# Identity products in the planned waits of TensorE, in a four-layer graph network

## The chip, the cores and the metric

The kernel runs on one core of a Trainium2 chip. The metric is the device time of one execution in microseconds, as the median of several runs. Five engines work side by side in the core: TensorE (matmul), VectorE (DVE), ScalarE (ACT), GpSimd (POOL) and SyncE (SP), which here only issues DMAs. They run their own instruction streams in order and wait for each other with semaphores.

## The reference

32 graphs of 512 nodes with 128 features pass through four layers; each is a graph network behind a layer norm and a ReLU, added to its input. Cut to what is computed:

```python
# layer 0
h = relu(layernorm(x)); A = adj + I; r = rowsum(A) ** -0.5
x = x + leaky_relu((r[:, None] * A * r[None, :]) @ (h @ W) + b, 0.01)
# layer 1
h = relu(layernorm(x))
x = x + tanh(concat(adj @ elu(h @ Win.T + bin), elu(h @ Wnode.T + bnode),
                    adj.T @ elu(h @ Wout.T + bout)) @ Wupd.T + bupd)
# layer 2: four steps, f0 = relu(layernorm(x)), with f1, f0 stashed and concatenated
f = tanh(concat(l2norm_rows(adj) @ (f @ ws + bs), f @ wn + bn,
                l2norm_cols(adj).T @ (f @ wd + bd)) @ wu + bu)
x = x + f4
# layer 3: a gated update
h = relu(layernorm(x)); m = tanh(adj @ (h @ Wmsg.T + bmsg))
r, z, n = gates(m, h)
x = x + (1 - z) * n + z * h
```

All is in float32, inputs, weights and products.

## The kernel before

A graph is a batch. Its adjacency matrix lies in SBUF twice, as it is (`a`) and transposed (`aT`), each as four chunks of 128 partitions by 512 columns. Aggregations are four accumulating products of 128x512, one for each chunk; weight products have 128 or 256 columns. Matrices that hang only on the weights are folded once, at the start (`ps_fold`, `ps_foldb`), and two-by-two blocks of products are written with seven instead of eight (`ps_seven`).

The kernel doesn't issue instructions while it walks through the layers. `program(b)` and `setup()` only record operations: engine, a duration assumed for it, what it reads and writes, and a closure that emits it. `Plan.order()` then simulates the five engines with these durations: an operation is ready when what it hangs on has ended, and each engine takes the ready one with the smallest key, which is a due time of its batch (28 us apart, `PERIOD`) less the length of the chain behind it. `order()` also hands out the eight PSUM banks and the SBUF slots. Its result is one list; emitting it in that order gives each engine its instruction stream. The real semaphores are put in later, from the data, so a stream's order is the plan's, but its times are the chip's.

The first batches run through the chain of layers with little else to do; from the third batch's start TensorE always has several batches to choose from. At the end, the last two batches are alone again. In batches 0 to 2, 30 and 31 the transposed h is made by TensorE (`transposed`, L483 with ACT's copy at L485); in the others by a DMA bounce (`turned`, copy at L488).

Names and lines that the text uses:

- Every matmul made by the helper `mm` has line L295, so tiles tell them apart: `ps_fold` and `ps_foldb` (weight folds, copied out by ACT at L353 and L371), `ps_agg` (aggregations), `ps_lin` (layer 0's weight, from `agg`, which ACT copies at L632), `ps_sd` (pairs of projections; DVE adds their bias at L522), `ps_node`, `ps_upd`, `ps_msg`, `ps_gate`. L566 is `ps_seven`.
- A layer norm is `bn`, `mv` and `v` on DVE (L419, L421, L422), the power on POOL (L435), `nb` on DVE (L443) and four activations `h` on ACT (L447), one for each 128 rows.
- Layer 0 ends with DVE's `z` (L637), `y` (L640) and `xr` (L642). Row sums come from ACT (`sq`, L607) and DVE's L609; sums of squares from ACT's L686, DVE's L689 and POOL's power L690, which goes through DRAM (`bounce`, L695, and `spaced`, L699) and ACT's `rows` (L704) into DVE's scaling of `aT` and `a` (L708).
- Layer 1's `rep` is ACT's exponential (L659) and DVE's L660 and L662; its outputs are copied by ACT as `agg_in` (L667) and `agg_out` (L671).
- Each step of layer 2 ends with ACT's tanh `f` (L737).
- The identity `ident` is made by POOL first thing; the products of the change read it.

Of the kernel before, what the change touches and what calls it, by code (L numbers as in the profile page):

```python
# [13 lines left out]
F32 = mybir.dt.float32  # L14
# [4 lines left out]
P = 128  # L19
B, N, D = 32, 512, 128  # L20
# [71 lines left out]
class Plan:  # L92
# [62 lines left out]
    def order(self):  # L155
        for i, o in enumerate(self.ops):
            o.waits, o.ready = len(o.after), 0.0
            for other in o.after:
                other.next.append(o)
            for buf in o.bufs:  # L160
                buf.left += 1
        for i, o in reversed(list(enumerate(self.ops))):
            o.tail = max([o.us + o.land] + [self.lag(o, n) + n.tail for n in o.next if n.batch == o.batch])

            due = o.batch * PERIOD if o.batch < B - 1 else (B - 2) * PERIOD + ENDING
            o.key = (due - o.tail + o.later if o.rank is None else o.rank - 1e6, i)
        free = {k: list(range(n)) for k, n in self.places.items()}
        unfinished = {}
        for o in self.ops:
            unfinished[o.batch] = unfinished.get(o.batch, 0) + 1  # L170
        queues, idle_at = {e: [] for e in self.SIGNAL}, dict.fromkeys(self.SIGNAL, 0.0)
        events, seq = [], 0

        def event(at, what, o=None):
            nonlocal seq
            seq += 1
            heapq.heappush(events, (at, seq, what, o))

        for o in self.ops:
            if not o.waits:  # L180
                event(0.0, "ready", o)
        done = []
        while events:
            now = events[0][0]
            while events and events[0][0] <= now + 1e-9:
                _, _, what, o = heapq.heappop(events)
                if what == "ready":
                    heapq.heappush(queues[o.engine], (o.key, o))
                elif what == "end":
                    for buf in o.bufs:  # L190
                        buf.left -= 1
                        if not buf.left and buf.kind in free:
                            free[buf.kind].append(buf.slot)
                    unfinished[o.batch] -= 1
                    if not unfinished[o.batch]:
                        del unfinished[o.batch]
            for e, queue in queues.items():
                if idle_at[e] > now + 1e-9:
                    continue
                held, o = [], None  # L200
                while queue and o is None:
                    item = heapq.heappop(queue)
                    new = [x for x in item[1].bufs if x.slot is None and x.kind in free]
                    older = item[1].batch - min(unfinished)
                    if any(len(free[x.kind]) < len([y for y in new if y.kind == x.kind]) + older * self.kept.get(x.kind, 0) for x in new):
                        held.append(item)
                        continue
                    o = item[1]
                    for x in new:
                        x.slot = free[x.kind].pop(0)  # L210
                for item in held:
                    heapq.heappush(queue, item)
                if o is None:
                    continue
                done.append(o)
                idle_at[e] = now + o.us
                event(now + o.us, "idle")
                event(now + o.us + o.land + self.SIGNAL[e], "end", o)
                for n in o.next:
                    n.waits -= 1  # L220
                    n.ready = max(n.ready, now + self.lag(o, n))
                    if not n.waits:
                        event(n.ready, "ready", n)
        assert len(done) == len(self.ops), "the plan does not end"
        return done


@with_exitstack
def gnn_stack(
# [11 lines left out]
    nc = tc.nc  # L241
    const = ctx.enter_context(tc.tile_pool(name="const", bufs=1))
    sb = ctx.enter_context(tc.tile_pool(name="sb", bufs=1))
    psum = ctx.enter_context(tc.tile_pool(name="psum", bufs=1, space=bass.MemoryType.PSUM))
    dram = ctx.enter_context(tc.tile_pool(name="dram", bufs=1, space=bass.MemoryType.DRAM))
    plan = Plan(sb, psum, {"bank": 8, "s2": 32, "s4": 6, "s8": 10}, {"bank": 1, "s2": 5, "s4": 0, "s8": 1})
# [7 lines left out]
    ident = const.tile([P, P], F32, name="ident")  # L254
# [133 lines left out]
    def program(b):  # L388
# [422 lines left out]
        for k in range(0, NC, w2):  # L811
            s, part, cols = slice(k, k + w2), set(range(k, k + w2)), w2 * D

            def step(dst, fn, reads, engine="DVE"):
# [12 lines left out]
            op("SP", 0.4, lambda s=s: nc.sync.dma_start(out[b][:, s, :], xo.ap()[:, s, :]),  # L827
               [(xo, part)], [], kb=cols / 2)

    setup()  # L830
    for b in range(B):
        program(b)
    with tc.manual_schedule():
        for o in plan.order():
            o.emit()


# [41 lines left out]
```

## Time and profile before

| what | value |
|---|---|
| median of 5 runs | 2330.21 us (2329.8 to 2331.43) |
| the profiled execution's own time | 2329.8 us |
| its span, first to last instruction | 2328.0 us |
| TensorE busy | 2294.4 us (99%) |
| DVE, ACT, POOL busy | 1520.0, 934.8, 287.6 us |
| mean granted TensorE clock | 0.996 |
| clock in 20 to 60 us, 60 to 100 us | 0.85, 0.98 |
| TensorE busy in 0 to 20 us, 20 to 60 us | 8.64, 31.68 us |
| TensorE's waits of over 2 us in all | the first fold for its load 10.7, transpositions for h 5.1 |

The profile is one execution, recorded by the hardware. A row of the timeline has start and duration in us, the engine, the line, the operation with its tiles and shapes, how many records were merged, and in brackets how long the engine had been idle before and what ended that. TensorE's ends are modelled: records overlap, so the pace of a stream is read from start to start. A float32 product has two matmul records (a transposition one), so "x8" is four products. A row of the windows has the stretch, its length, busy time and count of records of TensorE, its weight loads, DVE, ACT and POOL, then the granted clock, the DMA engines' mean share and GB/s.

### The profile page before, as it was taken

What the parts mean: (1) busy time and instruction counts of PE and PEld (TensorE: products, weight loads), DVE (VectorE), ACT (ScalarE), POOL (GpSimd) and SP (SyncE); (2) the same over time, 40 slices, a digit from 0 to 9 for tenths busy, and PEclk for the clock granted to TensorE, in tenths of its full rate; (3) what the DMA queues carried; (4) which work ended last, traced back from release to release, by engine and by line L of the source; (5) the groups of instructions that cost most, each with busy time, mean ns of one, the idle gap of its engine ahead of it and who ended that gap; (6) DMA issues with size and microseconds to landing.
All of it is one profiled execution on the core that took longest, in us unless ns stands there. A gap on an engine that the chain in (4) does not pass through costs nothing.

```text
span 2328.0 us, 28035 instructions
## 1 busy us (share of the span) xinstructions
PE 2294.4 (99%) x9594; PEld 1437.9 (62%) x9594; DVE 1520.0 (65%) x4124; ACT 934.8 (40%) x2018; POOL 287.6 (12%) x218
## 2 busy tenths in 40 slices
PE   6999999999999999999999999999999999999998
PEld 4666666566665666666666666666656666666665
DVE  5556567666676776757766676666767667576754
ACT  7323434344343444434444333443434444344512
POOL 2001101111110111111111111111001111111101
PEclk9999999999999999999999999999999999999999
DMA  6202222323323133222233223232231332323100
GB/s 219 78 1 86 68 74 80 109 64 100 98 84 109 47 108 105 91 86 88 75 101 100 77 88 109 64 100 93 82 114 48 109 97 93 92 63 114 50 5 10
DMA packets 127295, 196.63 MB, mean 84 GB/s; under 512 B 18352, under 2 KB 75184, under 8 KB 127152
## 3 DMA queue, kind: packets, MB, share of 16 engines
q1 hardware_dynamic: 126864, 194.71, 26.8%
q8 instruction: 76, 1.25, 0.2%
q14 instruction: 67, 0.55, 0.1%
q10 hardware_dynamic: 288, 0.13, 0.0%
HBM read 157.95 MB, written 36.83 MB: 84 GB/s over the span
## 4 chain that ended last, share of the span: by engine, by line
PE 90%; DVE 4%; DMA 3%; issue 2%; ACT 1%; POOL 1%; SPq 0%; ACTq 0%; DVEq 0%; POOLq 0%
PE ps_agg L295 60%; PE ps_seven L566 12%; PE ps_sd L295 9%; PE ps_upd L295 3%; PE ps_gate L295 2%; PE ps_msg L295 1%; PE ps_node L295 1%; PE ps_lin L295 1%; DMA turned<-turn_turned 0%; DMA aT<-in_adjt 0%; DVE bn L419 0%; ACT h L447 0%; DMA a<-in_adj 0%; POOL inv L690 0%; POOL sc L435 0%
## 5 line engine op out<-in xcount | busy, mean ns | idle before, releaser
L295 PE MATMUL ps_agg<-aT,sd 128*128 128x512 f32 x1024 | 510.0, 594 | 1.4 <-DVE sd L544 0.9
L295 PE MATMUL ps_agg<-a,sd 128*128 128x512 f32 x1024 | 489.4, 593 | 0.0
L435 POOL TENSOR_TENSOR sc<-v,neg_half 128x4 f32<-128x4 f32 (+1 forms) x128 | 173.7, 1358 | 1623.6 <-DVE v L422 1049.2
L295 PEld LDWEIGHTS ps_agg<-a,sd 128*128 128x128 f32 x1024 | 181.7, 190 | 158.3 <-issue 148.8
L447 ACT ACTIVATE h<-xr,nb,sc 128x128 f32<-128x128 f32 x384 | 158.2, 482 | 295.7 <-DVE nb L443 292.0
L295 PE MATMUL ps_agg<-f,w_sb 128*128 128x512 f32 x448 | 229.7, 595 | 0.0
L295 PEld LDWEIGHTS ps_agg<-aT,sd 128*128 128x128 f32 x1024 | 177.8, 191 | 74.8 <-issue 61.7
L295 PE MATMUL ps_sd<-w_sb,f 128*128 128x256 f32 x768 | 222.0, 382 | 1.4 <-ACT f L485 1.3
L566 PEld LDWEIGHTS ps_seven<-t_sb,s 128*128 128x128 f32 x1128 | 164.2, 191 | 67.9 <-issue 56.2
L295 PEld LDWEIGHTS ps_sd<-w_sb,f 128*128 128x128 f32 x768 | 137.7, 192 | 107.5 <-issue 86.4
L522 DVE TENSOR_TENSOR sd<-ps_sd,rf_sb 128x512 f32<-128x512 f32 x128 | 88.3, 690 | 149.9 <-PE ps_sd L295 149.2
L566 PE MATMUL ps_seven<-t_sb,s 128*128 128x128 f32 x1128 | 177.2, 275 | 0.0
L737 ACT ACTIVATE f<-ps_agg,cf_sb 128x512 f32<-128x512 f32 x128 | 87.4, 683 | 145.3 <-PE ps_agg L295 145.2
L295 PE MATMUL ps_agg<-aT,rep 128*128 128x512 f32 x256 | 130.9, 593 | 1.2 <-DVE rep L662 0.9
L295 PE MATMUL ps_agg<-a,rep 128*128 128x512 f32 x256 | 130.7, 592 | 0.0
L295 PE MATMUL ps_agg<-aT,msg 128*128 128x512 f32 x256 | 127.6, 593 | 0.0
L566 PEld LDWEIGHTS ps_seven<-w_sb,f 128*128 128x128 f32 x512 | 83.5, 191 | 55.7 <-issue 47.1
L690 POOL TENSOR_TENSOR inv<-stat,neg_half 128x8 f32<-128x8 f32 x32 | 64.7, 2021 | 372.1 <-DVE stat L689 372.1
L592 DVE TENSOR_TENSOR ev<-ps_seven,ev 128x512 f32<-128x512 f32 x94 | 64.7, 688 | 65.1 <-PE ps_seven L566 63.7
L295 PE MATMUL ps_agg<-aT,h 128*128 128x256 f32 (+2 forms) x384 | 99.7, 380 | 0.0
L607 ACT ACTIVATE sq<-a 128x512 f32<-128x512 f32 x128 | 79.9, 624 | 47.0 <-DMA a<-in_adj 45.4
L295 PEld LDWEIGHTS ps_agg<-f,w_sb 128*128 128x128 f32 x448 | 78.4, 191 | 27.8 <-issue 20.3
(142 smaller groups left out, 3781.6 us busy)
## 6 DMA issues: line engine op xcount, KB each, us to landing
aT<-in_adjt SPq DMA_DIRECT2D x124, 512.0 KB, 5.5
a<-in_adj SPq DMA_DIRECT2D x62, 512.0 KB, 5.2
turn_turned<-blk SPq DMA_DIRECT2D x324, 64.0 KB, 1.8
turned<-turn_turned SPq DMA_DIRECT2D x81, 256.0 KB, 2.6
spaced<-bounce SPq DMA_DIRECT2D x32, 512.0 KB, 4.7
x<-in_x SPq DMA_DIRECT2D x32, 256.0 KB, 2.7
out<-xo SPq DMA_DIRECT2D x30, 256.0 KB, 2.1
turn_f4r<-blk SPq DMA_DIRECT2D x108, 64.0 KB, 1.8
```

What stands on the lines that cost most here:

```text
L295: op("PE", t_mm(n), lambda: nc.tensor.matmul(out_of(ps.ap()), lhs(), rhs(), start=start, stop=stop), reads, [ps], later=later)
L435: op("POOL", t_pow(n), lambda: nc.gpsimd.tensor_tensor(inv.ap()[:, :n], v8.ap()[:, :n], neg_half[:, :n], op=ALU.pow), [v8, NH], [(inv, {0})])
L447: op("ACT", t_act(D, 2), lambda c=c: nc.scalar.activation(h.ap()[:, c, :], xin.ap()[:, c, :], AF.Relu, bias=nb.ap()[:, c:c + 1], scale=inv ...
L522: op("DVE", t_tt(N), lambda ps=ps, h=h: nc.vector.tensor_add(sd.ap()[:, 2 * h:2 * h + 2, :], ps.ap().rearrange("p (j v) -> p j v", j=2), s ...
L566: op("PE", t_mm(D), lambda j=j: nc.tensor.matmul(ps.ap()[:, k * H + j * D:k * H + (j + 1) * D], lhs()[:, j * P:(j + 1) * P], rhs(), start= ...
L592: op("DVE", t_tt(N), lambda: nc.vector.tensor_add(ev.ap(), bank_b.ap()[:, None, :H].to_broadcast([P, 2, H]), ev.ap()), [bank_b, ev], [ev])
L607: op("ACT", 0.73, lambda c=c: nc.scalar.activation(sq.ap(), a.ap()[:, c, :], AF.Copy, accum_out=stat.ap()[:, c:c + 1]), [(a, {c})], [sq, ( ...
L690: op("POOL", t_pow(2 * NC), lambda: nc.gpsimd.tensor_tensor(inv.ap(), stat.ap(), neg_half, op=ALU.pow), [stat, NH], [inv])
L737: op("ACT", t_act(N, 1), lambda ps=ps, i=i, f_new=f_new: nc.scalar.activation(f_new.ap(), ps.ap(), AF.Tanh, bias=cf_sb[:, i:i + 1]), [ps, ...
```

## The change

When the list of operations is complete, it is walked once more. Where TensorE's next operation starts, in the plan's time, more than 0.7 us after the last one ended, products of the identity with itself are put between them. Their number is the plan's gap divided by 0.428 us for the first 3.5 us of such gaps at the kernel's start, and by 0.2225 us afterwards. They write 128 columns of a PSUM bank which by the plan holds nothing in that gap, and nobody reads them. The identity is taken as ready at 1.3 us.

```diff
@@ order()
                         if not buf.left and buf.kind in free:
                             free[buf.kind].append(buf.slot)
+                            buf.until = now
...
-                        x.slot = free[x.kind].pop(0)
+                        x.slot, x.since, x.until = free[x.kind].pop(0), now, None
...
                 done.append(o)
+                o.ready = now
...
+    WARM, COLD, RISE, SHORT = 0.2225, 0.428, 3.5, 0.7
+
+    def kept_warm(self, done, product, begin):
+        banks = {x for o in done for x in o.bufs if x.kind == "bank"}
+        out, at, cold = [], begin, self.RISE
+        for o in done:
+            if o.engine == "PE":
+                gap = o.ready - at
+                if gap > self.SHORT:
+                    n = int(min(gap, cold) / self.COLD + max(gap - cold - 0.1, 0.0) / self.WARM)
+                    cold = 0.0
+                    used = {x.slot for x in banks if x.since < o.ready and x.until > at - 0.1}
+                    slot = next((k for k in range(self.places["bank"]) if k not in used), None)
+                    if slot is not None:
+                        out.append((slot, n))
+                at = o.ready + o.us
+            out.append(o)
+        for o in out:
+            if isinstance(o, tuple):
+                product(*o)
+            else:
+                o.emit()
...
+    def idle_products(slot, n):
+        ps = psum.tile([P, N], F32, name="ps_idle", tag=f"bank_{slot}", bufs=1)
+        for _ in range(n):
+            nc.tensor.matmul(ps[:, :P], ident, ident, start=True, stop=True)
+
     setup()
     for b in range(B):
         program(b)
     with tc.manual_schedule():
-        for o in plan.order():
-            o.emit()
+        plan.kept_warm(plan.order(), idle_products, 1.3)
```

The plan has twelve such gaps: nine in its first 53 us and three near its end, when batch 30 starts layer 2 and batch 31 leaves layer 0. They get 33, 3, 4, 5, 4, 5, 6, 14 and 4, and 5, 4 and 3 products, 90 in all. They stand ahead of these operations: the first `ps_fold`, the first `ps_lin`, the second and the third group of `ps_fold`, `ps_sd` of layer 1, `ps_agg` of layer 1, the second batch's `ps_lin`, the transpositions of layer 2's h, `ps_sd` of layer 2's first step; then the last `ps_lin`, the transpositions of batch 30's h, and its `ps_sd`. A bank's next user waits until the bank's last one is through: the first product of a group may wait for a reader on ACT or DVE, and the first fold, the third group of folds, `ps_agg` of layer 1, `ps_sd` of layer 2 and batch 30's transpositions wait for TensorE's own products ahead of them. The order of the instructions on DVE, ACT, POOL and SP is unchanged.

## The prediction

> **What bounds the kernel now.** I read the page first, then the clock in stretches of one microsecond, then the timeline of TensorE's instructions, engine by engine, where the clock was low.
>
> ```profile
> PE 2294.4 (99%) x9594; PEld 1437.9 (62%) x9594; DVE 1520.0 (65%) x4124; ACT 934.8 (40%) x2018; POOL 287.6 (12%) x218
> 27.00:28.00 1.00, 0.85 (x3) 0.28 (x2) 0.69 (x4) 1.00 (x4) 0.00 (x0) 0.90 0.79 262
> 28.00:29.00 1.00, 0.30 (x1) 0.30 (x2) 0.00 (x0) 1.00 (x4) 0.00 (x0) 0.50 0.83 279
> 34.00:35.00 1.00, 0.70 (x2) 0.37 (x2) 1.00 (x6) 0.78 (x2) 0.43 (x1) 0.69 0.99 397
> 55.00:56.00 1.00, 0.86 (x2) 0.32 (x2) 1.00 (x10) 1.00 (x4) 1.00 (x2) 0.55 0.23 60
> 61.00:62.00 1.00, 1.00 (x3) 0.48 (x2) 0.00 (x0) 1.00 (x5) 0.00 (x0) 0.53 1.05 401
> ```
>
> TensorE is the bound: of a span of 2328.0 us it idles some 34, and from 56.5 to 2179 us it waits less than 3 us in all. What its first matmuls of that stretch gain is therefore gained for the whole kernel. The third number from the right in the other rows is the granted clock. It falls at 27.8 (0.90 over one microsecond is a fifth of it at half speed), rises at 34.6, falls at 55.1 and rises at 61.9. Both low stretches last 6.8 us and the falls are 27.3 apart; all are multiples of 3.41, so a counter with that period decides, and a low stretch lasts until a whole period has been busy. From then to the last matmul the clock is full, so nothing can be won behind 62 us.
>
> ```profile
> 10.69 2.93 PE L295 MATMUL ps_fold<-raw 128*128 128x128 f32 x12 [10.69 <-DMA raw<-in_raw]
> 20.43 1.50 PE L295 MATMUL ps_fold<-raw 128*128 128x128 f32 x12
> 26.47 0.33 PE L483 MATMUL ps_t<-ident,h 128*128 128x128 f32 x1 [1.41 <-ACT h L447]
> 28.70 3.78 PE L295 MATMUL ps_sd<-w_sb,hT 128*128 128x256 f32 x8 [0.73 <-ACT hT L485]
> 34.48 1.17 PE L295 MATMUL ps_agg<-aT,rep 128*128 128x512 f32 x2 [0.30 <-DVE v L609]
> 54.23 1.63 PE L483 MATMUL ps_t<-ident,h 128*128 128x128 f32 x4 [3.08 <-ACT h L447]
> 56.53 2.08 PE L295 MATMUL ps_sd<-w_sb,f 128*128 128x256 f32 x4 [0.68 <-ACT f L485]
> 62.31 0.60 PE L295 MATMUL ps_sd<-w_sb,f 128*128 128x256 f32 x2
> 2179.99 1.16 PE L295 MATMUL ps_lin<-w_sb,agg 128*128 128x128 f32 x8 [0.68 <-ACT agg L632]
> 2195.97 1.10 PE L295 MATMUL ps_agg<-aT,rep 128*128 128x512 f32 x2 [0.93 <-DVE rep L662]
> ```
>
> The first two rows are the same work: twelve records take 2.71 us to the next row's start (13.40) at 10.69 and 1.34 at 20.43 (to 21.77). So the first folds run at half speed too, until about 14.2, though the page shows a full clock there. Each product is two records: 0.223 us at full clock, 0.45 at half.
>
> **The change, part by part.** 90 products are added on TensorE: 33, 3, 4, 5, 4, 5, 6, 14 and 4 in the first 60 us, and 5, 4 and 3 around 2180. The order on every other engine and in every DMA queue is the same. An added product costs its 0.223 or 0.45 us only where the wait it stands in is shorter than planned.
>
> *A, the 33 products ahead of the first fold.* They wait for the identity, which POOL finishes at 1.34. Half speed lasts one to two periods, 3.4 to 6.8 us (the trace's 3.5 and 6.8). That is 8 to 15 products, and the rest at 0.223: the end is at 10.5 to 12.1, with the trace's counter at 11.6. The first fold also waits for the last product to leave the array, 0.2 (a record's 0.275 less its share of the stream, 0.11). So the folds start at 11.8 instead of 10.69 but take 2.5 us instead of 4.3, ps_agg (3.57) ends at 17.9 instead of 18.75, and ACT's copy (L632), whose queue is free from 17.6, starts at 18.0 to 18.1 instead of 18.80. Between 0.3 (late counter) and 1.2 (ACT's queue) is won; I take 0.7. L637, which starts the chain to the next layer, starts when ps_lin ends.
>
> *B, the 4 and 5 products ahead of the second and third folds.* The plan has waits of 1.07 and 1.42 there, the trace none: the folds run back to back from 20.43. So 9 x 0.223 = 2.0 us of TensorE time is added. It lies beside DVE's and POOL's work on the layer norm (20.6 to 25.9): the folds end near 26.1 and the last transposition needs ACT's h, which with A ends at 26.9. I take nothing; without that cover it would be 2.0.
>
> *C, the 4 products ahead of ps_sd at 28.70, and 5 ahead of 34.48.* With B and these, TensorE streams ordinary products for at least 2.4 of any 3.41 us here. The trace keeps its clock in the period around 42 us with 2.0 to 2.2 busy, so I take it as kept. Eight ps_sd records then take 1.73 (2190.57 to 2192.30) instead of 3.57. The chain behind is ps_sd, DVE's add (30.81), ACT's exponential (31.54), DVE's L660 and L662, ps_agg at 34.48. The first add comes at 29.8; ACT is busy until 30.5 and again with a square until 31.65; L662 comes at 31.9 instead of 33.7. ps_agg starts 1.8 earlier; the two ends are 0, where the clock falls, and 1.9. The 5 products (1.1) fit behind ps_node. From 34.5 to 56.5 every step hangs on the one before (POOL's power behind L609, ACT's h, rows and agg_in, a dense DVE from 43.3 on); the loads they need land 5 us and more before, and spaced is issued behind POOL's power and moves along. So the 1.8 is kept.
>
> *The 6 and 14 products at 49.2 and 51.1.* Six take 1.34 in a wait of 0.84, so ps_lin ends 0.5 later, at 51.5; DVE reaches L637 only at 51.74. The 14 (3.1) then run to 54.7, half a microsecond past h's first chunk, but the transpositions follow h's chunks, the last of which comes at 55.4. Cost nothing; up to 0.5 if ACT were faster.
>
> *D, the 4 products ahead of 56.53.* ps_sd there waits for the last of them: 0.17. Then the work from 56.53 to 62.31 (four ps_sd records, two ps_agg, two ps_sd, two ps_agg) takes 0.87 + 0.86 + 0.43 + 0.86 = 3.01 instead of 5.78. Won: 2.6. DVE's add of the first half comes at 58.5 and is needed at 58.7.
>
> *What is late next.* TensorE is now 5.1 us ahead, ACT's queue only A + C = 2.5, and ACT is busy without a break from 57.9 to 65.5. Behind it stand h, a square and the tanh that ps_sd at 70.94 needs:
>
> ```profile
> 66.21 1.65 ACT L447 ACTIVATE h<-x,nb,sc 128x128 f32<-128x128 f32 x4 [0.60 <-DVE nb L443]
> 69.17 0.69 ACT L737 ACTIVATE f<-ps_agg,cf_sb 128x512 f32<-128x512 f32 x1 [0.70 <-PE ps_agg L295]
> ```
>
> ACT is free at 63.0, h and the square take it to 65.2, the tanh to 65.9; TensorE wants it at 65.8. I take 0.1 back, 1 at most.
>
> *Late, the 5, 4 and 3 products.* Five take 1.11 in a wait of 0.84 (2179.15 to 2179.99): ps_lin is 0.27 late, and with it L637, the layer norm, spaced, rows, rep and ps_agg at 2195.97, which waits for it. The other two fit. Cost 0.3, at most 0.5.
>
> **Sum**: -0.7 - 1.8 - 2.6 + 0.1 + 0.3 = -4.7 on the profiled execution's 2329.8 (2328.0 span and 1.8 around it): 2325.1. The median of the runs is 2330.2, 0.4 above, and part of that is the low stretches' place in the period, which the change mostly removes. **Predicted: 2325.2.** With the ends of all terms, 2323.8 to 2327.
>
> A rule speaks against C. The Trainium skill (TensorE: Matmul & The Clock Gate, "Why this matters for your kernels") holds that only gaps of some 3 us without matmuls bring the half clock back. By it the clock at 27.8 would not have fallen behind gaps of 1.41 and 0.73 us, C would have nothing to win, and the sum would be 2326.9. The trace's 0.50 at 28 us says otherwise. The same page ("Part 4: PE-mode transpose") says that transpositions don't count as activity, which fits: between 24.9 and 28.7 there is little else.
>
> **Rivals.**
> *One of C and D stays cold*, because the window with the transpositions is still too thin. For it: the periods from 27.8 and 55.1 were about 80% busy and did not raise the clock. Against it: those were about raising, and periods of 64% kept it. 2326.9 without C, 2327.6 without D.
> *ACT takes it back*: the tanh at 69.17 and what follows hold TensorE at ACT's lead of 2.5 us. 2327.6. For it the full ACT queue, against it 0.1 us of margin worked out above and an ACT that is mostly idle from 71 on.
> *Slower: the added products run at half speed throughout*, because identity products don't raise the clock. The first wait decides: 33 products fit into 9.3 us up to 0.28 each. At 0.45 they end at 16.3, folds 5.6 later; the 9 of B cost 4 us, 2.5 of it uncovered; the 14 take 6.3 in 4.2 with their cover, 2 more. Some 10 us: 2340. Against it: at 10.69 ordinary products of this very shape raised the clock in 3.5 us, and no row shows a dependence on the values.
>
> **How the numbers follow.** Forecast 0.73, one stretch cold 0.13, ACT 0.09, slower 0.05. About 0.2% (4.7 us) is what a measurement of this kernel tells from no change, so faster means under 2325.5. The forecast lies just below that line; I give 0.47 of its 0.73 to faster, the rest and the two middle rivals to same: 0.48. The range reaches from just under the forecast's low end to past the middle rivals: 2323.4 to 2328.4.
>
> **What would show it.** The clock at 1.00 in every stretch from 12 us to the last matmul; the first fold at 10.7 to 12.3 with 0.223 a product; ps_sd's eight records in 1.73; the place that was at 62.31 reached near 57.2; f (L737) within 0.2 us of its ps_sd; no wait shown ahead of the last ps_lin. It is wrong if a 0.50 stands anywhere between 20 and 60, if TensorE waits for L737 near 65 for over 1 us, or if the products of the first wait take over 0.28 each.

## The result, and the profile after

The changed kernel takes 2326.45 us in the median of 25 runs (2324.99 to 2331.39); the kernel before took 2330.85 us beside it (2329.13 to 2334.01, 45 runs). The ratio is 0.9982, with a 95% interval of 0.9977 to 0.9987: 4.4 us by the medians, 0.18% by the ratio, are won. 2325.2 was forecast. The gain is just under the 0.2% (4.7 us) that the prediction took for what a measurement tells from no change, but the interval lies wholly under 1. A second measurement gave 2327.77 against 2332.25, ratio 0.9981 (0.9972 to 0.9990). The profiled execution took 2325.31 us, its span is 2323.5 us and its mean granted clock 0.999: 4.5 us under the profile of before. Lines of the changed kernel are those of before plus 29.

The page's line of busy times, of the changed kernel:

```profile
PE 2308.2 (99%) x9774; PEld 1455.4 (63%) x9774; DVE 1519.6 (65%) x4124; ACT 934.1 (40%) x2018; POOL 286.6 (12%) x218
```

Its windows, with the granted clock third from the right:

```profile
27.00:28.00 1.00, 0.95 (x8) 0.80 (x8) 0.56 (x3) 1.00 (x4) 0.00 (x0) 1.00 0.69 254
28.00:29.00 1.00, 1.00 (x7) 0.90 (x7) 0.00 (x0) 1.00 (x4) 0.00 (x0) 1.00 0.94 307
55.00:56.00 1.00, 1.00 (x6) 0.68 (x5) 0.95 (x4) 1.00 (x4) 0.00 (x0) 1.00 1.06 144
```

Its timeline of TensorE:

```profile
1.40 10.02 PE L862 MATMUL ps_idle<-ident 128*128 128x128 f32 x66 [1.40 <-POOL ident masks.py:199]
11.47 1.60 PE L324 MATMUL ps_fold<-raw 128*128 128x128 f32 x12
...
23.82 2.27 PE L324 MATMUL ps_fold<-raw 128*128 128x128 f32 x18
...
28.28 1.99 PE L324 MATMUL ps_sd<-w_sb,hT 128*128 128x256 f32 x8
...
32.31 1.12 PE L324 MATMUL ps_agg<-aT,rep 128*128 128x512 f32 x2
...
54.55 1.10 PE L324 MATMUL ps_sd<-w_sb,f 128*128 128x256 f32 x4
...
57.63 0.59 PE L324 MATMUL ps_sd<-w_sb,f 128*128 128x256 f32 x2
...
2175.40 1.06 PE L324 MATMUL ps_lin<-w_sb,agg 128*128 128x128 f32 x8
...
2191.53 1.10 PE L324 MATMUL ps_agg<-aT,rep 128*128 128x512 f32 x2 [1.55 <-DVE rep L691]
```

TensorE is busy for 14 us more and the kernel is 4.5 us shorter: nearly all that was added stands in waits. No 0.50 is left up to the last matmul (the clock falls at 2320.7 us, 5 us behind it). Place by place the lead over the profile of before is 0.84 at the first layer's `z` (20.63 to 19.79), 0.42 at `ps_sd` (28.70 to 28.28), 2.17 at `ps_agg` (34.48 to 32.31), 1.98 at layer 2's first `ps_sd` (56.53 to 54.55), 4.68 at the place that was at 62.31, 4.59 at the last `ps_lin` and 4.44 at the last layer-1 `ps_agg`. Between `z` and `ps_sd` 0.42 is lost. DVE's `z` before and after, and ACT's timeline before and after, show where:

```profile
20.63 1.13 DVE L637 SCALAR_TENSOR_TENSOR z<-ps_lin,sc,r_sb 128x128 f32<-128x128 f32 x4 [5.28 <-DMA a<-in_adj]
23.53 0.59 ACT L353 COPY w_sb<-ps_fold 128x512 f32<-128x512 f32 x1 [0.63 <-PE ps_fold L295]
25.92 1.65 ACT L447 ACTIVATE h<-xr,nb,sc 128x128 f32<-128x128 f32 x4 [1.80 <-DVE nb L443]
```

```profile
19.79 1.13 DVE L666 SCALAR_TENSOR_TENSOR z<-ps_lin,sc,r_sb 128x128 f32<-128x128 f32 x4 [5.28 <-PE ps_lin L324]
25.02 0.59 ACT L382 COPY w_sb<-ps_fold 128x512 f32<-128x512 f32 x1 [2.07 <-PE ps_fold L324]
25.50 1.65 ACT L476 ACTIVATE h<-xr,nb,sc 128x128 f32<-128x128 f32 x4
```

ACT's copy of the third folds, which began at 23.53 before, waits 2.07 us for TensorE, and `h`, which waited for DVE's `nb` before, now stands behind the copy in ACT's queue.

### The profile page after: what moved, and what is told of

The parts are those of the page before. It is cut to its first block, busy times and chain, and to the rows that moved or that the text cites. A ratio compares the mean times of both kernels' runs of the same rounds, so it can differ in the third digit from the quotient of the medians.

```text
span 2323.5 us, 28393 instructions
## 1 busy us (share of the span) xinstructions
PE 2308.2 (99%) x9774; PEld 1455.4 (63%) x9774; DVE 1519.6 (65%) x4124; ACT 934.1 (40%) x2018; POOL 286.6 (12%) x218
## 3 DMA queue, kind: packets, MB, share of 16 engines
q8 instruction: 77, 1.26, 0.2%
## 4 chain that ended last, share of the span: by engine, by line
PE 95%; DVE 2%; DMA 1%; ACT 1%; SPq 0%; POOL 0%; issue 0%; DVEq 0%; POOLq 0%; ACTq 0%
PE ps_agg L324 63%; PE ps_seven L595 12%; PE ps_sd L324 9%; PE ps_upd L324 4%; PE ps_gate L324 2%; PE ps_msg L324 1%; PE ps_lin L324 1%; PE ps_node L324 1%; PE ps_idle L862 1%; ACT h L476 0%; DMA turned<-turn_turned 0%; SPq L494 0%; DVE bn L448 0%; DMA turn_turned<-blk 0%; PE ps_t L512 0%
```

## The experiments

Each was one edit of the changed kernel. What follows is read above all from one place, the start of the eight `ps_agg<-a,sd` records that end layer 2's first step, because the stretch from there to the last `ps_lin` differs between executions of one program. The table has it for every profiled execution, with the medians of all runs; each of the three groups of experiments was timed on one chip. "Stretch" is the time from the eight records to the last `ps_lin`.

| kernel | first fold | eight records | last `ps_lin` | stretch | median | before | ratio |
|---|---|---|---|---|---|---|---|
| before | 10.69 | 65.53 | 2179.99 | 2114.5 | 2330.85 | | |
| changed | 11.47 | 60.86 | 2175.40 | 2114.5 | 2326.45 | 2330.85 | 0.9982 (0.9977 to 0.9987) |
| --- | | | | | | | |
| first 33 only | 10.99 | 63.22 | 2181.52 | 2118.3 | 2331.24 | 2331.72 | 0.9996 (0.9987 to 1.0006) |
| without the folds' 4 and 5 | 11.33 | 61.80 | 2176.89 | 2115.1 | 2326.75 | 2331.72 | 0.9978 (0.9969 to 0.9987) |
| without the late 5, 4, 3 | 10.61 | 62.69 | 2177.87 | 2115.2 | 2328.66 | 2331.72 | 0.9986 (0.9977 to 0.9995) |
| 14 and 4 only | 10.82 | 64.06 | 2179.31 | 2115.3 | 2329.36 | 2331.72 | 0.9991 (0.9982 to 1.0001) |
| --- | | | | | | | |
| changed, again | 11.36 | 60.74 | 2177.54 | 2116.8 | 2327.77 | 2332.25 | 0.9981 (0.9972 to 0.9990) |
| with 6 ahead of `ps_upd` | 11.93 | 61.35 | 2179.52 | 2118.2 | 2326.21 | 2332.25 | 0.9974 (0.9964 to 0.9984) |
| refined, 30 first | 10.49 | 59.53 | 2175.44 | 2115.9 | 2325.06 | 2332.25 | 0.9973 (0.9964 to 0.9983) |
| 14 and 4 as transpositions | 10.69 | 60.29 | 2175.98 | 2115.7 | 2327.33 | 2332.25 | 0.9981 (0.9972 to 0.9990) |
| --- | | | | | | | |
| first 33 as transpositions | 10.92 | 63.05 | 2178.20 | 2115.2 | 2328.46 | 2332.26 | 0.9985 (0.9976 to 0.9994) |
| refined, 26 first | 10.63 | 59.67 | 2175.47 | 2115.8 | 2325.31 | 2332.26 | 0.9973 (0.9964 to 0.9983) |
| refined, 30 first, again | 10.78 | 59.47 | 2176.89 | 2117.4 | 2325.05 | 2332.26 | 0.9972 (0.9962 to 0.9982) |
| without the first 33 | 10.34 | 61.80 | 2176.83 | 2115.0 | 2329.87 | 2332.26 | 0.9991 (0.9982 to 0.9999) |

The stretch varies by 3.8 us, almost as much as the change wins. TensorE's clock is full there, and its bracketed waits in it add up to 2.1 to 4.8 us. One of them, in ACT's timeline of the kernel with 6 ahead of `ps_upd`, and the same copy in the refined kernel:

```profile
425.16 0.62 ACT L522 COPY hT<-turned 128x512 f32<-128x512 f32 x1 [5.45 <-DMA turned<-turn_turned]
```

```profile
421.48 0.62 ACT L523 COPY hT<-turned 128x512 f32<-128x512 f32 x1 [3.66 <-DMA turned<-turn_turned]
```

From the end of DVE's `blk<-f` (417.49 and 415.52) the DMA's way to memory and back took 7.67 us in the first and 5.96 in the second, and `ps_sd` waited 1.24 us for it in the first only. Such round trips are one source of the scatter. It needs no edit: the stretches of two executions of one program differ by 2.3 us (changed) and 1.5 us (refined).

**Each group alone, and each taken away.** A counter of the groups, `seen`, picks which get products.

```diff
+        seen = 0
...
+                    n, seen = n if seen == 0 else 0, seen + 1
...
-                    if slot is not None:
+                    if slot is not None and n:
```

The condition is `seen == 0` (the first 33 only), `seen not in (2, 3)` (without the folds' 4 and 5), `seen < 9` (without the late ones), `seen in (7, 8)` (14 and 4 only) and `seen > 0` (without the first 33).

> Only the 33 products ahead of the first fold; the other 57 are left out. My theory (each stretch's clock is held by the products that stand in it): z (the first one, DVE after ps_lin) comes 0.85 us earlier, h of layer 1 0.85 earlier too, the clock falls near 25 to 28 and near 52 to 55 as in the kernel before, and the time is 0.6 to 1.2 us under the kernel before. Rival (once the clock is up early, the short waits that follow do not bring it down): the clock stays at 1.00 and the time is 4 us or more under the kernel before.

The mechanism held; the time can't be told from no change (0.9987 to 1.0006). `z` comes 1.09 us earlier than before instead of 0.85. Windows of the granted clock of the kernel with the first 33 only:

```profile
28.00:29.00 1.00, 1.00 (x5) 0.86 (x4) 0.04 (x1) 1.00 (x4) 0.00 (x0) 0.72 0.89 242
53.00:54.00 1.00, 1.00 (x3) 0.36 (x2) 1.00 (x10) 1.00 (x4) 1.00 (x2) 0.50 0.19 22
```

The clock falls near 28 and near 52 us as in the kernel before, against the rival: a warm start is not carried to the next thin stretch. It fell at 2185 us too, where the profile of before shows it full.

> All but the 4 and 5 products ahead of the second and third group of folds. Theory 1 (they only cost, through ACT's copy of the third folds that stands ahead of h): h comes at 25.1 instead of 25.5, the clock stays at 1.00, ps_sd's eight records still take 1.73, and the time is 0.4 under the changed kernel. Theory 2 (they also hold the clock, since without them the period around 24 to 28 us has little but transpositions): the clock falls near 25 to 28, the eight records take 3.4 to 3.7, and the time is 1.2 to 1.6 above the changed kernel, 2.8 to 3.3 under the kernel before.

Each theory held in part. Without the nine, `h` starts at 24.94 us and waits for DVE instead of the copy, 0.56 earlier than in the changed kernel (0.14 of it is the first fold's earlier start): they cost 0.42. But they also hold the clock. Windows of this kernel:

```profile
26.00:27.00 1.00, 0.89 (x4) 0.51 (x5) 0.71 (x4) 1.00 (x3) 0.00 (x0) 0.81 0.81 274
27.00:28.00 1.00, 1.00 (x7) 1.00 (x7) 0.00 (x0) 1.00 (x4) 0.00 (x0) 0.50 0.83 299
```

And its timeline of TensorE, the four products ahead of `ps_sd`:

```profile
26.91 1.91 PE L864 MATMUL ps_idle<-ident 128*128 128x128 f32 x8
```

The clock falls at 26.6, the four products ahead of `ps_sd` take 1.91 us instead of 1.06, and the eight records start at 61.80, 0.94 later than in the changed kernel. The eight `ps_sd` records take 2.43 us, not the 3.4 to 3.7 of theory 2, since the clock is back near 30. The median, at 5.0 us under before instead of 2.8 to 3.3, does not show that loss; the intervals overlap.

> All but the 5, 4 and 3 products near the end. My theory: the last ps_lin starts 0.27 earlier after its ps_agg, ps_agg's wait for rep shrinks from 1.55 to 1.1, and the end comes 0.3 to 0.45 earlier than in the changed kernel. Rival (what follows there waits for loads and other engines anyway): the end moves by less than 0.1.

The cost is there, but the time is not: 3.1 us under the kernel before, where the changed kernel won 4.4. `z` of the last layer 0 starts 2.26 us after the last `diag` product and 2.43 in the changed kernel, so the late products cost 0.17. The clock fell in the stretch behind them, and it fell at 42 us as well, in a wait that the change leaves empty. Windows of the kernel without the late ones:

```profile
42.00:43.00 1.00, 1.00 (x6) 1.00 (x7) 1.00 (x3) 1.00 (x4) 0.00 (x0) 0.58 0.00 0
...
2183.00:2184.00 1.00, 1.00 (x3) 0.50 (x2) 0.54 (x2) 0.00 (x0) 0.82 (x1) 0.50 0.83 207
```

POOL's timeline of it, the power for the second batch's first layer norm and row sums:

```profile
31.71 3.28 POOL L466 TENSOR_TENSOR sc<-v,neg_half 128x8 f32<-128x8 f32 x1 [7.52 <-DVE v L640]
```

And TensorE's, the first `ps_upd`:

```profile
41.88 0.56 PE L326 MATMUL ps_upd<-w_sb,agg_in 128*128 128x128 f32 x2 [2.22 <-ACT agg_in L698]
```

POOL's power took 3.28 us in this execution and 1.94 in the changed kernel's profile, so that batch's `h`, and `agg_in` behind it in ACT's queue, came a microsecond later, counted from `ps_agg`, and TensorE waited 2.22 instead of 1.24 us. Why the power took longer is open. The plan sees less than 0.7 us there and puts no products. In the profiles of all three kernels on this chip that have no late products the clock fell (at 2182.3, 2183.8 and 2185.7 us); in the profile of before, which has none either, it did not.

> Only the 14 and 4 products around the transpositions of layer 2's h (51 to 56 us). My theory: the low stretch near 28 to 34 stays as in the kernel before, the one near 55 to 62 is gone, the work from the first ps_sd there to the fifth pair of records takes 3.0 to 3.2 instead of 5.8, and the time is 2.3 to 2.6 under the kernel before. Rival (ACT, which is not ahead here, holds the tanh after it): TensorE waits near 69 us and the time is 1 to 2 under the kernel before.

As the theory said, with a median 2.4 us under before (interval 0.9982 to 1.0001): the work from `ps_sd` on that took 5.78 us before takes 3.09 (57.75 to 60.84), the clock falls from 30 to 33 us, and TensorE does not wait for `f` near 69.

> The changed kernel without the 33 products ahead of the first fold, all other products kept. Theory (they are worth the half-speed stretch of the folds and ps_agg, less ACT's and the copy's share): the first fold at 10.5 to 11 at half speed, ps_lin of the first layer at 19.4 to 20.6 instead of 18.5, ps_agg<-a,sd at 61.7 to 62.9, so 0.8 to 2 us over the changed kernel: 2.4 to 3.6 under the kernel before. Rival (the copy of the third folds, and not the first folds, sets when h starts, so nothing is lost): ps_agg<-a,sd at 60.7 to 61.3, 4 us or more under the kernel before.

The theory held, at its lower edges (61.8 and 2.4 us under before). TensorE's timeline of this kernel shows the first fold at half speed:

```profile
10.34 2.93 PE L326 MATMUL ps_fold<-raw 128*128 128x128 f32 x12 [10.34 <-DMA raw<-in_raw]
```

`ps_lin` starts at 19.52 us instead of 18.59 and the eight records at 61.80, 0.94 later than in the changed kernel, though `raw` landed 0.35 earlier than in the profile of before. The medians against their own kernels before differ by 2.1 us (2.4 and 4.5 won), with overlapping intervals. That profile is its fastest run; in the kernel with 14 and 4 only the same cold folds led to a `ps_lin` at 20.53, a microsecond later, though `raw` landed only 0.48 later. There the pace rose near 16 us, here before 15. So what the 33 win depends on how long the folds run at half speed, and that differs between executions.

**Whether the changed kernel's gain holds, and the wait ahead of `ps_upd`.**

> The changed kernel once more, unaltered, on the same chip as the next three. Theory (the gain is the warm stretches at 0, 28 and 56 us, less 0.4 at the third folds and 0.2 to 0.4 at the late z): 4.0 to 4.9 us under the kernel before. Part of its executions lose 0.7 to 1.8 us because the clock falls in the wait ahead of ps_upd near 41 us, so its single times spread over 2 us or more. Rival (the first measurement was luck of the chip): under 3 us of gain.

4.5 us by the medians: it holds. The spread (2326.71 to 2329.35) is there, but the clock of this profile is full near 41 us, and the stretch behind, 2.3 us longer than in the first profile, explains it as well.

```diff
+                if not filled and any(x.name == "ps_upd_0" for x in o.bufs):
+                    filled = True
+                    used = {x.slot for x in banks if x.since <= o.ready + 1.5 and x.until > at - 0.1}
+                    out.append((next(k for k in range(self.places["bank"]) if k not in used), 6))
-                if gap > self.SHORT:
+                elif gap > self.SHORT:
```

> The changed kernel and six products more, in the wait of 1.24 us ahead of the first ps_upd, which the plan takes for too short. Theory (in a share of the executions the clock falls in this wait, as in the run without the late products, 2.22 us of wait and 0.50 at 43 us): median 0.3 to 1.5 us under the changed kernel, a narrower spread, clock 1.00 from 36 to 48 us. Rival (the wait is too short to matter when the first products are there): the changed kernel's time within 0.3 us, or 0.1 more for the six products of 1.34 us in a wait of 1.24.

Inconclusive. The median is 1.6 us under the changed kernel's, but the intervals overlap, the spread is not narrower (2324.56 to 2329.11), and its profile is its slowest run, for the stretch of 2118.2. The six products did no harm: from `ps_agg` to `ps_upd` 9.27 us pass, 9.24 in the changed kernel. The clock was full at 42 us in all four profiles with these six, and fell in two of the seven that have the 33, or 66 transpositions, ahead of the first fold but not the six: those two in which the wait was 2.2 us.

**The refined kernel.** To the six ahead of `ps_upd` come 30 instead of 33 first products, none ahead of the second folds, and banks that the next operation does not use, so that no product of TensorE holds up the next one.

```diff
-                    used = {x.slot for x in banks if x.since < o.ready and x.until > at - 0.1}
+                    n, seen = {0: 30, 2: 0}.get(seen, n), seen + 1
+                    used = {x.slot for x in banks if x.since <= o.ready + 1e-6 and x.until > at - 0.1}
```

> As the kernel with the ps_upd wait filled, but 30 instead of 33 products ahead of the first fold, none ahead of the second folds, and the products in a bank that the next operation does not use. Theory (the 0.43 us that ACT's copy of the third folds costs h comes from the four products ahead of the second folds and the late first fold; each self-wait is 0.17 to 0.23): z at 19.2 to 19.6 instead of 19.79, h of layer 1 at 24.9 to 25.2 instead of 25.50, ps_sd at 27.7 to 28.0, no wait of TensorE for itself; 0.5 to 1.2 us under the kernel with the ps_upd wait filled. Rival (what is won there is lost to POOL's power, which takes 1.9 or 3.3 us by what DVE does beside it, or the clock falls near 24 us): no gain over it, and POOL's sc at its old time.

> The refined kernel with 30 once more, beside the one with 26. Theory: ps_agg<-a,sd at 59.4 to 60.2, 5.5 to 7.3 us under the kernel before. Rival (its first result was scatter of the 2115 us behind 61 us): under 4.9 us, the changed kernel's gain.

The theory held twice, and in its mechanism. ACT's timeline of the first of the two:

```profile
23.13 0.59 ACT L388 COPY w_sb<-ps_fold 128x512 f32<-128x512 f32 x1 [1.74 <-PE ps_fold L330]
24.41 1.65 ACT L482 ACTIVATE h<-xr,nb,sc 128x128 f32<-128x128 f32 x4 [0.69 <-DVE nb L478]
```

`h` now waits for DVE and not for the copy, and starts 1.09 earlier than in the changed kernel, before the 24.9 to 25.2 expected, as `z` does (19.11). The eight records start at 59.53 and 59.47, 1.3 earlier than in the changed kernel. Part of that is a first fold that starts earlier; the kernel without the late products has the same `z` (19.13) with all nine fold products, and its `h` starts at 24.84, so the freed copy is worth 0.4. The medians are 2325.06 and 2325.05, 7.2 under the kernel before, by the ratios 6.3 and 6.5 (0.9973, 0.9972); eight of nine runs lie below the fastest run of the changed kernel on the same chip.

> The refined kernel with 26 instead of 30 products ahead of the first fold. Theory (half speed lasts 3.3 to 6.2 us from the first product, by where the counter stands, so 33 products overrun the load of raw at 10.5 to 10.7 in most executions and 30 in some): 26 end at 8.8 to 10.7, the first fold starts at 10.4 to 10.8 in every execution, ps_agg<-a,sd at 59.4 to 59.8, median 0 to 0.6 us under the refined kernel with 30. Rival (a gap of up to 1.8 us ahead of the fold lets the clock fall in the first folds): ps_agg<-a,sd at 60.3 or later, 0.5 to 2 us slower than with 30.

A wash: 59.67, and 2325.31 beside 2325.05. The folds ran at full speed behind the 1.26 us between the products and the load, against the rival; but with 30 the folds started at 10.49 and 10.78, about when the load lands, so little was left to win.

**Do transpositions hold the clock?** The prediction leaned on the rule that they do not.

```diff
-        for _ in range(n):
-            nc.tensor.matmul(ps[:, :P], ident, ident, start=True, stop=True)
+        for _ in range(2 * n if turn else n):
+            if turn:
+                nc.tensor.transpose(ps[:, :P], ident, ident)
+            else:
+                nc.tensor.matmul(ps[:, :P], ident, ident, start=True, stop=True)
```

`turn` is true for the groups of 14 and 4 in one kernel, for the 33 in the other.

> The changed kernel with the 14 and the 4 products of the last early wait (51 to 56.5 us) as 28 and 8 transpositions of the identity. Theory (transpositions do not count as activity): the clock is 0.50 in the stretch behind, from near 55 to 62 us, ps_sd at 54.6 takes about 2.1 instead of 1.1 us for four, and 2.3 to 2.6 us of the gain are lost: 2 to 2.4 us under the kernel before. Rival (any stream through the array counts): the clock stays 1.00, four ps_sd in 1.1 us, the changed kernel's time within 0.4 us.

The rival was right. TensorE's timeline of that kernel:

```profile
48.63 3.22 PE L865 MATMUL ps_idle<-ident 128*128 128x128 f32 x28
51.69 1.26 PE L514 MATMUL ps_t<-ident,h 128*128 128x128 f32 x4
52.79 1.04 PE L865 MATMUL ps_idle<-ident 128*128 128x128 f32 x8
53.98 1.10 PE L326 MATMUL ps_sd<-w_sb,f 128*128 128x256 f32 x4
```

A window of it, with the `ps_sd` behind:

```profile
54.00:55.00 1.00, 1.00 (x5) 0.90 (x6) 0.93 (x5) 1.00 (x3) 0.06 (x1) 1.00 0.75 144
```

For 5.2 us nothing but transpositions runs, and the clock stays full. Since a period of 3.41 us might still have had other work at its edges, the first wait was tried, where nothing else runs for 9 us:

> The changed kernel with the 33 products ahead of the first fold as 66 transpositions of the identity; from a cold start nothing else runs on TensorE for 9 us. Theory (a transposition counts as activity, as the run with 36 transpositions near 50 us suggests): the clock rises during them, they end at 10.5 to 12 us, the first twelve fold records take 1.6 us, the eight ps_agg<-a,sd records start at 60.2 to 61.4 as in the changed kernel, 3.5 to 5 us under the kernel before. Rival (transpositions do not count, and there ordinary products held the clock): 66 at half speed end near 16.1, the folds behind run at half speed too, the eight records start 4 us later or more, and the time is that of the kernel before or above it.

TensorE's timeline of this kernel:

```profile
1.40 9.32 PE L865 MATMUL ps_idle<-ident 128*128 128x128 f32 x66 [1.40 <-POOL ident masks.py:199]
10.92 1.58 PE L326 MATMUL ps_fold<-raw 128*128 128x128 f32 x12 [0.20 <-DMA raw<-in_raw]
...
42.23 0.49 PE L326 MATMUL ps_upd<-w_sb,agg_in 128*128 128x128 f32 x2 [2.23 <-ACT agg_in L698]
```

And a window of it, a microsecond behind the `ps_upd`:

```profile
43.00:44.00 1.00, 1.00 (x7) 1.00 (x7) 1.00 (x3) 1.00 (x5) 0.00 (x0) 0.50 0.00 0
```

66 transpositions take 9.32 us. By the starts of the single records in the trace they come 0.213 us apart at first and 0.109 from 5.3 us on; all at the first pace they would take 14.1. They raised the clock, and the folds behind them ran at full speed. The median, 3.8 us under before, is inside the 3.5 to 5 expected. The eight records of this profile start late, at 63.05, for another reason than either theory had: POOL's power took 3.29 us, the wait ahead of `ps_upd` 2.23, and the clock fell at 42.9, for one period.

## Why the prediction was right, and where not

The sum was -4.7 and the profiles differ by -4.5. The mechanism was right, but that the two agree to 0.2 is partly luck: the stretch from the eight records to the last `ps_lin` happened to be 2114.5 us in both profiles, and it was 2.3 us longer in the changed kernel's second one. By the medians 4.4 us were won, where the forecast had 5.0 (2330.2 to 2325.2). The terms, as measured between the two profiles:

- **A, the first wait**: -0.7 forecast, -0.84 at `z`. The 33 ran into the load's arrival by 0.8 us as foreseen. By the starts of the single records in the trace a product takes 0.427 us while cold (0.45 in the sum) and 0.2235 behind, and half speed lasted 5.1 us; in the other profiles with a filled first wait 2.9 to 6.0, where 3.4 to 6.8 were assumed. The short ones, 2.9 to 3.2 us in four profiles, are under one period of 3.41, so "until a whole period has been busy" is too strict. The size is that of one pair of executions: against the run without the 33 it was 0.94 by the profile and some 2 us by the medians.
- **B, the folds' 4 and 5**: forecast 0, measured +0.42. This step failed, as the sum put it: "the folds end near 26.1 and the last transposition needs ACT's h, which with A ends at 26.9. I take nothing". The cover was looked for on TensorE and DVE, and not in ACT's queue, where the copy of the third folds stands ahead of `h`. Without the nine, and in the refined kernel, which drops four of them, `h` waits for DVE's `nb` again. That these products also hold the clock was taken for granted in C's step ("With B and these") and is shown by the fall at 26.6 without them.
- **C, `ps_sd` of layer 1**: -1.8 forecast; the lead grows from 0.42 to 2.17, -1.75. Eight records take 1.83 us from start to start.
- **D, layer 2's first step**: -2.6 forecast; from `ps_sd` to the place that was at 62.31, 3.08 instead of 5.78 us, less 0.23 in which `ps_sd` waits for the last product: -2.47.
- **ACT behind it**: +0.1 forecast, 0 measured: the lead is 4.68 at 57.63 and at the `ps_sd` that was at 70.94.
- **Late**: +0.3 forecast; the last `ps_lin` loses 0.28 of the lead. But "so nothing can be won behind 62 us" was read from one execution. In three others without the late products the clock fell there, so these products are not a cost alone. How much they win cannot be told: from the last `ps_lin` to the last layer-1 `ps_agg` 15.8 to 16.9 us pass, in kernels with and without them, by how long the way of `bounce` and `spaced` through memory takes (from `bounce`'s issue to ACT's `rows`, 7.42 us at the low end and 8.47 at the high one).

The ends given as 2323.8 to 2327 do not come out of the terms. With all of them at their best (A 1.2, C 1.9, D 2.6, nothing lost) it is 2324.1; with C at the 0 that its step allows, A at 0.3, ACT at 1 and the late products at 0.5 it is 2328.4, without the 0.5 of the 14 and the 2.0 of B.

Of the rivals, a cold C or D appeared in neither profile of the changed kernel; half speed throughout fell with the first row, 33 products in 10.02 us instead of 14.1; ACT took nothing back. What none of them named is the wait ahead of `ps_upd`, which was seen to lose the clock for 3.4 us twice.

One sign of being wrong did show by its letter: the products of the first wait took 0.30 us each (10.02 us for 33), over the 0.28 that was named. The sign was set too low, for the sum's own end of the 33, at 10.5 to 12.1 us, means 0.28 to 0.32 each; the pace did rise. The place that was at 62.31 came at 57.63 instead of near 57.2, which is in the main B's 0.42.

The Trainium skill ("TensorE: Matmul & The Clock Gate", "Why this matters for your kernels") allows gaps of some 3 us. The trace does not agree: the clock fell behind waits of 2.22 and 2.23 us, and at 26.6, without the folds' nine, behind one of 1.41 and transpositions that wait for `h`. Behind the waits of 1.23 to 1.29 ahead of `ps_upd` it stayed. (In the kernel before, too, only the wait of 1.41 stands ahead of the fall at 27.8; the 0.73 that the prediction names with it begins later.) The same page's "Part 4: PE-mode transpose", that transpositions do not count, was called fitting in the prediction. It was the wrong reading: transpositions raised the clock from cold and held it for 5.2 us. By that the fall at 27.8 before comes from the waits around and between them.

## What to carry to other kernels

A thin stretch loses the clock each time anew, so each is worth its own filling, and of a filling it matters less how many products it has than that none of them is late for the work behind it: fewer products, in a bank which the next operation does not use, and one more wait filled, won some two microseconds more by the ratios (1.3 by the places), all three together. When work is added to an engine that looks idle, follow its results into the queues of the engines that drain it; what stands behind the drain is late too. And before a few microseconds are put down to an edit, compare places ahead of the long stretch that the edit doesn't touch: that stretch alone varied by 3.8 us here.

## What the runs showed of the hardware

- A 128x128 float32 product of the identity with itself, whose result nobody reads, raises TensorE's pace as other products do, from 0.427 to 0.2235 us each; so do transpositions of the identity, from 0.213 to 0.109 us each.
- The first half-speed stretch lasted 2.9 to 6.0 us from the first product or transposition, by execution, and the page shows a full clock during it. Later low stretches last one or two periods of 3.41 us: by the windows 42.9 to 46.3 us in the run with 66 transpositions, 28.4 to 31.8 and 52.3 to 59.2 with the first 33 only.
- POOL's power on 128x8 elements took 1.94 us in most profiles and 3.28 us in two, in the same place of the same program order, and a microsecond of it reached TensorE's wait.
